# A residual layer with a split fp32 product on one Trainium2 core: another place in the order for stores, for one cast of W and for two products

## Chip, cores and metric

The kernel runs on one core of one Trainium2 chip. The metric is the device time of one execution in microseconds (us), as the median of several runs. Lower is better.

## What is computed

The reference, cut to what matters (B = 4 rows, L = 1024, D = 512, `cond` has 256 columns, W is 1536 x 512):

```python
hidden = concatenate([cond, cond], axis=-1)                    # (4, 512)
x_mean = mean(x, axis=1, keepdims=True)                        # (4, 1, 512)
fused = concatenate([x, x_mean * ones_L, hidden[:, None, :] * ones_L], axis=-1)
relation = relu(einsum('bld,do->blo', fused, W) + b)
out = x + relation
```

The first 512 rows of W multiply x itself. The other 1024 rows multiply something that is the same for all 1024 positions of a row of the batch, so the kernel computes that part once for each of the four rows, as a bias of 512 numbers.

## The kernel before

**Tiles.** x is cut into 32 tiles t of 128 positions by 512 columns, eight to a batch row. A product tile needs x transposed, in four chunks j of 128 columns. To get fp32 accuracy, x and W are both split into a high part and a rest, `hi` and `lo`, `w_hi` and `w_lo`, and each chunk takes three matmuls (task `p{t}.{j}.{n}`, L365): n = 0 is hi by w_hi, n = 1 lo by w_hi, n = 2 hi by w_lo. That makes 12 matmuls of 512 columns for a tile, collected in one of five PSUM banks `po`. `p{t}.{j}` is all three at once.

**Where the parts come from.** The four chunks of W arrive in buffer x0 (tasks `W0` to `W3`); ScalarE's queue issues the first, SyncE the others. `wh{j}` (L218 on VectorE, L216 on ScalarE) casts a chunk to w_hi, `wl{j}` (L222) subtracts to get w_lo. For the first four tiles TensorE makes the transposes itself (`T{u}.{j}`, L262) from a regrouped copy (`y`, L237 or L235); for the later ones VectorE transposes blocks of a second load of x (`Z` loads into buffers z, transposes L264). `h{u}.{j}` on ScalarE (L271) casts to hi and adds up the sums that the mean needs, as an ACTIVATE and a read of its accumulator. `l{u}.{j}` (L277) on VectorE or GpSimd subtracts to get lo.

**The way out.** A finished bank is copied to a buffer `o` (`K`, L432, L430 or L440), gets its bias (`b`, L436 on GpSimd) and the relu (`r`, L447 on ScalarE), and is added to the plain x tile (`F`, L454, on GpSimd or VectorE). The last four tiles start their banks from the bias and finish in one step on VectorE (`F`, L423, and the halves of the last tile `F31r`, `F31l`, L403). `S{t}` stores the tile from the x buffer.

**Plain x and its buffers.** `X{g}.{h}` loads pairs of plain tiles for the final addition. Eight groups g of four tiles share six buffers: group 6 goes where group 0 was, and group 7 where group 1 was. So X6.0 has to wait until the stores S0 and S1 have landed, X6.1 for S2 and S3, X7.0 for S4 and S5, X7.1 for S6 and S7.

**Order.** Nothing is scheduled automatically. The table `ORDER` (from L22) lists every task, and each engine issues its tasks in just that order, with semaphore waits between engines. An engine that waits holds back everything behind it. All `X`, `Z`, `M`, `S` tasks and W1 to W3 are DMAs that SyncE issues (L146), in one queue. The program gives eight semaphores to the DMAs in turn, so that an issue also waits for the landing of the one eight places ahead of it.

Of the kernel before, what the change touches and what calls it, by code (L numbers as in the profile page):

```python
# [21 lines left out]
ORDER = """  # L22
W0@a X0.0 fill X0.1 relu fill X0.2 fill W1 fill W2 fill fill W3 fill y0.2@d y0.0@d X0.3 y0.1@d fill Z4.0 wh0r@d T0.0
fill wh0l@d h0.0 T0.2 wl0r@d Z4.1 T0.3 T0.1 p0.0.0 y1.0@d h0.2 Z4.3 wl0l@d y1.1@a T1.0 T1.1 l0.0@d h0.1 p0.0.2
y2.0@d Z4.2 y2.1@a T1.2 p0.0.1 h1.0 T1.3 T2.0 h1.1 T2.2 l1.0@d T2.1 wh1@d T2.3 p1.0.2 h2.1 p1.0.1 wl1@d h2.3 p1.1.0
p0.1.0 h1.3 wh2@d p1.0.0 h1.2 p0.1.2 l0.2@d h0.3 p1.2.0 l1.2@d h2.0 l2.1@d p2.1.2 wh3@a l2.3@d p2.1.0 Z5.3 l0.1@d
p1.1.2 l2.0@d p1.2.1 wl2@d p0.2.1 p2.1.1 y3.0@a p2.3.0 wl3@d p1.3.0 Z5.2 h2.2 p0.1.1 l1.1@d p0.3.0 l0.3@d p1.2.2
l1.3@d p0.3.2 l2.2@d p2.3.2 p1.1.1 Z5.0 p2.0.2 p1.3.1 T3.2 p2.0.0 T3.3 p2.3.1 p2.2.0 Z5.1 p2.2.1 p2.2.2 T3.0 T3.1
p0.2.2 h3.0 p2.0.1 h3.3 p0.2.0 C l3.0@d p1.3.2 h3.1 B p3.0 h3.2 l3.1@d K1@a l3.3@d V l3.2@d p3.1 T4.0 K2@a M1 T4.1
p3.2 h4.0 M0 h4.1 p0.3.1 l4.0@d p3.3 T4.2 l4.1@p p6.0 M3 T4.3 h4.2 p7.0 K0@a l4.2@d p4.1 h4.3 M2 p6.2 l4.3@p p4.0  # L30
Z6.3 T5.2 Z6.0 p5.0 to0 T5.1 Z6.2 K3@d p4.2 h5.1 t2 p7.2 as0 T5.0 h5.2 p6.3 t3 T5.3 h5.0 p5.1 h5.3 l5.0@d Z6.1 ac0@p
p7.3 t0 l5.2@d p4.3 ac1@p t1 p6.1 c0.0 K4@a Z8.1 p5.3 l5.3@p c0.1 p9.0 Z7.2 m0.0 p5.2 l5.1@p m0.1 p8.2 Z7.3 K5@a
m0.2 K6@a p8.3 m0.3 p10.0 Z7.1 p11.1 f0 p8.1 Z7.0 fa0 p11.0 vh0 T6.3 p11.2 X4.1 vl0 h6.3 X2.1 p10.1 T6.2 l6.3@p p7.1
Z8.0 T6.1 pb0 T6.0 p8.0 bc0@a Z8.2 as1 p9.1 b5@p K8@d h6.2 p9.2 Z8.3 h6.1 l6.2@d p9.3 b0@p h6.0 c1.0 p10.3 K7@a Z9.1
c1.1 to1 p13.2 K9@a l6.1@p m1.0 p13.3 l6.0@d p11.3 b3@p T7.1 p13.1 K11@a m1.1 r0@a p14.1 Z9.2 b1@p m1.2 h7.1 p10.2
T7.0 p14.0 X1.0 b4@p K10@a X1.1 T7.3 h7.0 p14.2 m1.3 l7.1@p Z9.0 p15.1 l7.0@d f1 p12.2 h7.3 fa1 b6@p p13.0 T7.2 vh1
p16.0 l7.3@p Z10.3 h7.2 vl1 p14.3 Z9.3 r1@a T8.1 p12.1 F0@p T8.0 h8.1 Z10.0 p15.2 T8.3 pb1 b7@p l7.2@d p16.3 bc1@a
as2 p15.3 K13 h8.3 F1@p p12.0 T8.2 r7@a p12.3 X3.1 h8.0 b8@p X2.0 p18.1 h8.2 K12 S0 p18.2 r3@a c2.0 to2 Z10.2 r4@a
p17.3 b2@p c2.1 r8@a p18.0 m2.0 F3@p p18.3 r2@a K14 r5@a p17.1 m2.1 r12@a l8.3@p S3 p16.1 m2.2 Z10.1 p17.2 X5.1 m2.3
F2@p p19.1 S1 l8.0@d f2 p15.0 l8.1@p r6@a fa2 p17.0 K15 X4.0 vh2 p19.2 F5@p T9.0 p19.3 vl2 h9.0 p19.0 F4@p T9.1  # L40
p20.1 l8.2@d b11@p pb2 p16.2 bc2@a h9.1 p20.2 K16 b10@p as3 p20.3 T9.2 p20.0 K17 h9.2 l9.1@p p21.2 r13@a l9.2@d
r17@a p22.0 T9.3 F7@p X6.0 K18 p21.1 h9.3 X3.0 S5 c3.0 F8@p p22.3 r10@a S4 T10.2 p21.0 S2 S7 K20 l9.3@p p21.3 h10.2
X5.0 l9.0@d r18@a p23.2 T10.1 F6@p p23.0 T10.3 p25.1 K21 b9@p h10.3 p22.2 T10.0 h10.1 p23.3 c3.1 h10.0 X6.1 p26.0
X7.0 r15@a F18@d r9@a p25.3 to3 K19 F10@p r14@a p22.1 m3.0 r19@a p26.3 m3.1 F9@p p26.2 m3.2 p24.1 m3.3 F17@p S9
p25.2 S6 K22 f3 S18 p24.0 F12@p S8 fa3 p25.0 vh3 F19@d p23.1 r20@a X7.1 F13@p p24.3 r22@a S10 K23 S17 p27.1 vl3
r23@a l10.3@p p26.1 l10.0@d r11@a pb3 F23@d p27.2 bc3@a F11@p l10.2@d S23 P28 p27.0 S19 K25 p24.2 S12 F15@p K26 P30
S11 p28.0 K24 P31l p27.3 r16@a F22@d S15 P29 S13 p30.3 F14@p r21@a S22 p28.2 r26@a F21@d S14 p28.3 l10.1@p K27 S21
p29.3 r27@a p29.2 F26@d r25@a p29.0 F20@d P31r S26 r24@a F27@d p30.1 S20 F25@d p28.1 S27 F24@p S25 p31.2l F28 p29.1
S28 F16@p p31.0l F29 p31.3l p30.0 S29 S24 p30.2 S16 p31.1r F30 p31.3r p31.2r S30 p31.0r p31.1l F31r F31l S31r S31l
""".split()  # L50


# [436 lines left out]
```

## Time and profile before

| what | value |
|---|---|
| median of 3 runs | 103.57 us |
| the three runs | 103.57, 104.98, 101.28 us |
| the profiled execution: its time | 101.22 us |
| the profiled execution: span from first to last instruction | 99.5 us |
| TensorE (PE) busy | 95.0 us, 96% of the span |
| VectorE (DVE), ScalarE (ACT), GpSimd (POOL) busy | 80.2, 58.2, 65.1 us |
| granted TensorE clock | full in all 40 slices |
| moved by DMA | 27.36 MB, 275 GB/s on the mean |

The profiled execution takes 1.7 us more than its span. PE is TensorE's matmuls, PEld its weight loads, SP is SyncE. The times in a row of the timeline count from the span's start.

### The profile page before, as it was taken

To read this page: it belongs to the slowest core of one execution; us is meant where nothing else is said; L and a number is where in the kernel's file an instruction comes from. 1 tells how busy PE (TensorE), PEld (TensorE's weight loads), DVE (VectorE), ACT (ScalarE), POOL (GpSimd) and SP (SyncE) were. 2 spreads that over 40 slices of the span, in tenths; PEclk is the share of its full clock that TensorE was granted. 3 is DMA by queue.
4 is the path that set the end of the run, shared out by engine and by line. 5 is a ranking of instruction groups with operands and counts; after the bars stand their busy time and mean duration, and the time that the engine had idled before them with its cause. 6 is when DMAs were issued, how large, how long until landed. Compare 5 with 4: busy or idle time off the path is not lost.

```text
span 99.5 us, 1446 instructions
## 1 busy us (share of the span) xinstructions
PE 95.0 (96%) x425; PEld 76.2 (77%) x425; DVE 80.2 (81%) x144; ACT 58.2 (58%) x153; POOL 65.1 (65%) x65
## 2 busy tenths in 40 slices
PE   6999999999999999999999999999999999999960
PEld 2466888778888888888888888888888888888850
DVE  1559807999897967999988999799999989699550
ACT  4297308659316549487899745677593587952000
POOL 5000000549940249999999999999979999967400
PEclk9999999999999999999999999999999999999999
DMA  2999999999999999999999999848999589999993
GB/s 43 376 375 239 210 199 212 278 394 314 222 209 212 215 254 269 209 223 275 259 212 242 328 294 268 308 133 264 390 315 366 208 275 285 404 406 406 398 385 123
DMA packets 25361, 27.36 MB, mean 275 GB/s; under 512 B 1413, under 2 KB 16009, under 8 KB 25354
## 3 DMA queue, kind: packets, MB, share of 16 engines
q1 hardware_dynamic: 25210, 27.01, 100.8%
q10 hardware_dynamic: 144, 0.26, 0.7%
q8 instruction: 3, 0.05, 0.2%
q14 instruction: 4, 0.03, 0.1%
HBM read 18.88 MB, written 8.39 MB: 274 GB/s over the span
## 4 chain that ended last, share of the span: by engine, by line
PE 93%; ACT 2%; DVE 1%; issue 0%
PE po L365 87%; PE po L132 4%; ACT hi L271 1%; PE acc L343 1%; DVE x L403 1%; ACT o L235 1%; PE po L262 0%; DVE lo L277 0%; PE acc L262 0%; PE px L262 0%; DVE warm L123 0%; DVE one L124 0%
## 5 line engine op out<-in xcount | busy, mean ns | idle before, releaser
L365 PE MATMUL po<-w_hi,lo 128*128 128x512 f32 (+1 forms) x132 | 50.6, 386 | 0.1
L365 PE MATMUL po<-w_lo,hi 128*128 128x512 f32 (+1 forms) x132 | 50.5, 385 | 0.0
L365 PE MATMUL po<-w_hi,hi 128*128 128x512 f32 (+1 forms) x132 | 50.4, 386 | 0.0
L277 POOL TENSOR_TENSOR lo<-xT,hi 128x512 fp32r<-128x512 f32 x14 | 18.6, 1335 | 23.5 <-ACT hi L271 23.5
L365 PEld LDWEIGHTS po<-w_hi,lo 128*128 128x128 f32 x132 | 24.9, 188 | 5.7 <-DVE lo L277 0.7
L365 PEld LDWEIGHTS po<-w_hi,hi 128*128 128x128 f32 x132 | 24.7, 188 | 5.3 <-issue 0.4
L365 PEld LDWEIGHTS po<-w_lo,hi 128*128 128x128 f32 x132 | 24.8, 188 | 4.7
L454 POOL TENSOR_TENSOR x<-o,x 128x512 f32<-128x512 f32 x19 | 26.3, 1406 | 1.5 <-ACT o L447 1.5
L447 ACT ACTIVATE o<-o 128x512 f32<-128x512 f32 x28 | 16.2, 620 | 1.6 <-DVE o L440 1.3
L436 POOL TENSOR_TENSOR o<-o,bias 128x512 f32<-128x512 f32 x12 | 15.5, 1309 | 1.4 <-ACT bias L347 1.4
L271 ACT ACTIVATE hi<-px 128x512 fp32r<-128x512 f32 (+1 forms) x20 | 9.9, 495 | 4.9 <-DVE px L264 2.6
L319 DVE SCALAR_TENSOR_TENSOR acc<-w_mean,tot,acc 128x512 f32<-128x512 f32 x16 | 12.0, 750 | 0.6
L440 DVE TENSOR_TENSOR o<-po,bias 128x512 f32<-128x512 f32 x16 | 10.7, 677 | 1.7 <-PE po L365 1.7
L277 DVE TENSOR_TENSOR lo<-px,hi 128x512 fp32r<-128x512 f32 (+1 forms) x20 | 10.9, 558 | 1.1 <-ACT hi L271 1.0
L271 ACT ACTIVATE hi<-xT 128x512 fp32r<-128x512 f32 x14 | 8.8, 627 | 3.0 <-DVE xT L264 3.0
L264 DVE STREAM_TRANSPOSE px<-z 128x512 f32<-128x512 f32 x14 | 9.9, 707 | 0.0
L264 DVE STREAM_TRANSPOSE xT<-z 128x512 f32<-128x512 f32 x14 | 9.6, 690 | 0.2
L432 ACT ACTIVATE o<-po 128x512 f32<-128x512 f32 x10 | 5.6, 599 | 5.6 <-PE po L365 5.6
L454 DVE TENSOR_TENSOR x<-o,x 128x512 f32<-128x512 f32 x9 | 8.0, 914 | 0.9 <-ACT o L447 0.9
L303 DVE SCALAR_TENSOR_TENSOR acc<-wc,cT,acc 128x512 f32<-128x512 f32 x8 | 6.0, 746 | 0.3
L132 PE MATMUL po<-warm 128*128 128x512 bf16 x9 | 4.1, 614 | 1.0 <-DVE one L124 1.0
L327 ACT ACTIVATE fold<-acc 64x512 f32<-64x512 f32 x4 | 2.4, 597 | 4.4 <-DVE acc L319 4.4
(53 smaller groups left out, 59.4 us busy)
## 6 DMA issues: line engine op xcount, KB each, us to landing
out_dram<-x SPq DMA_DIRECT2D x31, 256.0 KB, 4.0
z<-in_x_dram SPq DMA_DIRECT2D x28, 256.0 KB, 8.0
x<-in_x_dram SPq DMA_DIRECT2D x14, 512.0 KB, 6.5
x<-in_x_dram SPq DMA_DIRECT2D x4, 256.0 KB, 3.9
x<-in_L_cond_W_dram SPq DMA_DIRECT2D x1, 1024.0 KB, 7.6
w_mean<-in_L_cond_W_dram SPq DMA_DIRECT2D x4, 256.0 KB, 7.4
x<-in_L_cond_W_dram SPq DMA_DIRECT2D x3, 256.0 KB, 4.1
x<-in_L_cond_W_dram ACTq DMA_DIRECT2D x1, 256.0 KB
```

Of the source, the lines that this page charges most:

```text
L132: nc.tensor.matmul(ps_o[2], lhsT=warm, rhs=warm.rearrange("p (o d) -> p o d", o=1).to_broadcast([P, 4, P]), start=True, stop=True,)
L264: nc.vector.transpose(xT.rearrange("p (n q e) -> p n q e", q=Q // E, e=E), zs[z_of(u)][:, : n * NQ].rearrange("p n (q j e) -> p n j q e", ...
L271: nc.scalar.activation(his[buf][:, col : col + m], xT, AF.Copy, accum_out=sums[:, r, j, s : s + 1])
L277: nc_of[e].tensor_tensor(los[buf][:, col : col + m], xT, his[buf][:, col : col + m].bitcast(F32), ALU.subtract)
L303: nc.vector.scalar_tensor_tensor(acc, wc[:, k], cT[:, k, r : r + 1], acc, ALU.mult, ALU.add)
L319: nc.vector.scalar_tensor_tensor(acc, w_mean[:, j, :], tot[:, r, j : j + 1], acc, ALU.mult, ALU.add)
L365: nc.tensor.matmul(v, lhsT=a[:, col : col + P], rhs=m, start=WAYS[t] != "I" and key not in done, stop=done.count(key) == 3 * J - 1, skip_g ...
L432: nc.scalar.activation(o, bank(t), AF.Copy)
L436: nc_of[e].tensor_tensor(o, o, biases[r], ALU.add)
L440: nc.vector.tensor_tensor(o, bank(t), biases[r], ALU.add)
L447: nc.scalar.activation(o, o, AF.Relu)
L454: nc_of[e].tensor_tensor(x_tile(t), o, x_tile(t), ALU.add)
```

## The change

Only the table `ORDER` is changed. It has 28 lines instead of 27, so all later code stands one line further down.

- On VectorE, `wh1` (the cast of W's second chunk to w_hi) stands ahead of `l1.0` (lo of tile 1's first chunk) instead of behind it.
- On TensorE, `p1.1.0` and `p0.1.0`, which need that w_hi, stand ahead of `p1.0.1`, which needs that lo.
- On SyncE, stores from S2 on stand in the order in which their tiles are finished. S2, S5 and S4 stand ahead of the loads X6.0 and X3.0; X5.0, X6.1 and X7.0 stand behind S7 as before; of the later stores several change places with each other, and X7.1 now stands behind S8, S6, S18 and S10.

In the text of the table every store moves to just behind its `F`, which moves it on SyncE only where it passes another DMA.

```diff
-fill wh0l@d ... h1.1 T2.2 l1.0@d T2.1 wh1@d T2.3 p1.0.2 h2.1 p1.0.1 wl1@d h2.3 p1.1.0
-p0.1.0 h1.3 wh2@d p1.0.0 ...
+fill wh0l@d ... h1.1 T2.2 wh1@d l1.0@d T2.1 T2.3 p1.0.2 h2.1 p1.1.0 p0.1.0 p1.0.1
+wl1@d h2.3 h1.3 wh2@d p1.0.0 ...
...
-... X4.0 vh2 p19.2 F5@p ... F4@p ... F7@p X6.0 ... X3.0 S5 c3.0 F8@p ... S4 ... S2 S7 ... X5.0 ... X6.1 ... X7.0 ...
+... X4.0 S2 vh2 p19.2 F5@p S5 ... F4@p S4 X6.0 X3.0 ... F7@p S7 X5.0 X6.1 X7.0 ... F8@p S8 ...
```

VectorE near 6 us of the program, before: a copy for tile 2's transposes (`y2.0`), lo of tile 1 chunk 0, then the casts and subtractions of W's chunks 1 and 2.

```order
L237 COPY o10_115<-x2_65 128x256
L277 TENSOR_TENSOR lo1_91<-acc_143,hi1_76 128x128
L218 CAST w_hi_72<-x0_63 128x512
L222 TENSOR_TENSOR w_lo_73<-x0_63,w_hi_72 128x512
L218 CAST w_hi_72<-x0_63 128x512
```

And after:

```order
L238 COPY o10_115<-x2_65 128x256
L219 CAST w_hi_72<-x0_63 128x512
L278 TENSOR_TENSOR lo1_91<-acc_143,hi1_76 128x128
L223 TENSOR_TENSOR w_lo_73<-x0_63,w_hi_72 128x512
L219 CAST w_hi_72<-x0_63 128x512
```

The first cast has passed the subtraction that makes lo; the rest stands as it did.

TensorE at the same place, before: from `p1.0.2` to `p1.2.0` (po1 and hi1 are tile 1's, po0 and hi0 tile 0's).

```order
L365 MATMUL po1_137<-w_lo_73,hi1_76 128x512
L365 MATMUL po1_137<-w_hi_72,lo1_91 128x512
L365 MATMUL po1_137<-w_hi_72,hi1_76 128x512
L365 MATMUL po0_136<-w_hi_72,hi0_75 128x512
L365 MATMUL po1_137<-w_hi_72,hi1_76 128x512
L365 MATMUL po0_136<-w_lo_73,hi0_75 128x512
L365 MATMUL po1_137<-w_hi_72,hi1_76 128x512
```

And after:

```order
L366 MATMUL po1_137<-w_lo_73,hi1_76 128x512
L366 MATMUL po1_137<-w_hi_72,hi1_76 128x512
L366 MATMUL po0_136<-w_hi_72,hi0_75 128x512
L366 MATMUL po1_137<-w_hi_72,lo1_91 128x512
L366 MATMUL po1_137<-w_hi_72,hi1_76 128x512
L366 MATMUL po0_136<-w_lo_73,hi0_75 128x512
L366 MATMUL po1_137<-w_hi_72,hi1_76 128x512
```

The product with lo has gone from second to fourth place, and two products with the moved cast's w_hi stand ahead of it.

SyncE from X4.0 to X7.0, before (x2 is the buffer of tiles 0 to 3 and later of 24 to 27, x3 that of tiles 4 to 7 and later of 28 to 31, x5 that of tiles 12 to 15, x1 of tiles 20 to 23):

```order
L146 DMA x0_63<-in_x_dram 128x2x512
L146 DMA x2_65<-in_x_dram 128x2x512
L146 DMA x5_68<-in_x_dram 128x2x512
L146 DMA out_0_dram<-x3_66 128x512 x2
L146 DMA out_0_dram<-x2_65 128x512
L146 DMA out_0_dram<-x3_66 128x512
L146 DMA x1_64<-in_x_dram 128x2x512
L146 DMA x2_65<-in_x_dram 128x2x512
L146 DMA x3_66<-in_x_dram 128x2x512
```

And after:

```order
L147 DMA x0_63<-in_x_dram 128x2x512
L147 DMA out_0_dram<-x2_65 128x512
L147 DMA out_0_dram<-x3_66 128x512 x2
L147 DMA x2_65<-in_x_dram 128x2x512
L147 DMA x5_68<-in_x_dram 128x2x512
L147 DMA out_0_dram<-x3_66 128x512
L147 DMA x1_64<-in_x_dram 128x2x512
L147 DMA x2_65<-in_x_dram 128x2x512
L147 DMA x3_66<-in_x_dram 128x2x512
```

Three stores of 256 KB (S2, S5, S4) have passed two loads of 512 KB (X6.0, X3.0); S7 and the three loads behind it keep their places.

## Rows read from the trace of the kernel before

**Rows 1.** The page's busy times, and its DMA slices (40 slices of 2.49 us)

```profile
PE 95.0 (96%) x425; PEld 76.2 (77%) x425; DVE 80.2 (81%) x144; ACT 58.2 (58%) x153; POOL 65.1 (65%) x65
...
DMA  2999999999999999999999999848999589999993
```

**Rows 2.** The chain that ended last: start us, us, what

```profile
7.43 5.61 PE po L365 x22
...
49.85 12.92 PE po L365 x57
...
82.26 13.43 PE po L365 x69
...
95.72 0.78 DVE x L403 x2
```

**Rows 3.** Timeline of VectorE from 5.6 us: start us, us, what [idle before]

```profile
5.71 0.28 DVE L237 COPY o<-x 128x256 f32<-128x256 f32 x1
7.09 0.29 DVE L277 TENSOR_TENSOR lo<-acc,hi 128x128 fp32r<-128x128 f32 x1 [1.10 <-ACT hi L271]
7.30 0.42 DVE L218 CAST w_hi<-x 128x512 fp32r<-128x512 f32 x1
7.75 0.69 DVE L222 TENSOR_TENSOR w_lo<-x,w_hi 128x512 fp32r<-128x512 f32 x1
8.36 0.42 DVE L218 CAST w_hi<-x 128x512 fp32r<-128x512 f32 x1
```

**Rows 4.** Timeline of TensorE's matmuls from 6.8 us

```profile
6.90 0.48 PE L365 MATMUL po<-w_lo,hi 128*128 128x512 f32 x1
7.43 0.50 PE L365 MATMUL po<-w_hi,lo 128*128 128x512 f32 x1
7.86 0.94 PE L365 MATMUL po<-w_hi,hi 128*128 128x512 f32 x3
8.64 0.39 PE L365 MATMUL po<-w_lo,hi 128*128 128x512 f32 x1
8.93 0.47 PE L365 MATMUL po<-w_hi,hi 128*128 128x512 f32 x1
```

**Rows 5.** Timeline of ScalarE: the read of the accumulator that ends `h1.1`

```profile
6.84 0.21 ACT L271 ACTIVATION_READ_ACCUMULATOR hi<-acc 128x1 f32 x1
```

**Rows 6.** SyncE's issue of W1 to W3, and W's time from issue to landing

```profile
2.10 1.92 SPq L146 DMA_DIRECT2D x<-in_L_cond_W_dram  x3
...
x<-in_L_cond_W_dram SPq DMA_DIRECT2D x3, 256.0 KB, 4.1
```

**Rows 7.** SyncE's queue: its longest waits (us in total, times, longest)

```profile
SPq L146 <- DMA out_dram<-x: 9.6, 4, 4.8
SPq L146 <- POOL x L454: 6.9, 5, 2.8
...
SPq L485 <- DMA out_dram<-x: 1.3, 1, 1.3
```

**Rows 8.** Stretches: us, then busy us (x instructions) by engine, PEclk, DMA share, GB/s

```profile
64.00:66.00 2.00, 2.00 (x10) 1.66 (x9) 1.82 (x4) 1.59 (x6) 2.00 (x3) 1.00 0.32 88
...
77.00:79.20 2.20, 2.20 (x12) 1.81 (x11) 2.13 (x4) 0.94 (x2) 2.20 (x3) 1.00 0.51 187
...
82.00:97.00 15.00, 14.04 (x74) 11.89 (x72) 11.89 (x18) 6.29 (x12) 9.69 (x7) 1.00 1.03 379
97.00:98.20 1.20, 0.00 (x0) 0.00 (x0) 0.00 (x0) 0.00 (x0) 0.00 (x0) 1.00 0.74 254
```

**Rows 9.** X7.1, loads of 512 KB (us to landing), the last issue (S31l), the addition of tile 30

```profile
80.47 0.39 SPq L146 DMA_DIRECT2D x<-in_x_dram  x1
...
x<-in_x_dram SPq DMA_DIRECT2D x14, 512.0 KB, 6.5
...
96.60 0.40 SPq L146 DMA_DIRECT2D out_dram<-x  x1
...
94.29 0.69 DVE L423 SCALAR_TENSOR_TENSOR x<-po,x 128x512 f32<-128x512 f32 x1 [1.02 <-PE po L365]
```

More of the change, by code (lines that the diff above doesn't have):

```diff
@@ L24 @@
 fill wh0l@d h0.0 T0.2 wl0r@d Z4.1 T0.3 T0.1 p0.0.0 y1.0@d h0.2 Z4.3 wl0l@d y1.1@a T1.0 T1.1 l0.0@d h0.1 p0.0.2
[L25 to L48, printed above, removed]
@@ L49 @@
-S28 F16@p p31.0l F29 p31.3l p30.0 S29 S24 p30.2 S16 p31.1r F30 p31.3r p31.2r S30 p31.0r p31.1l F31r F31l S31r S31l
+y2.0@d Z4.2 y2.1@a T1.2 p0.0.1 h1.0 T1.3 T2.0 h1.1 T2.2 wh1@d l1.0@d T2.1 T2.3 p1.0.2 h2.1 p1.1.0 p0.1.0 p1.0.1
+wl1@d h2.3 h1.3 wh2@d p1.0.0 h1.2 p0.1.2 l0.2@d h0.3 p1.2.0 l1.2@d h2.0 l2.1@d p2.1.2 wh3@a l2.3@d p2.1.0 Z5.3
+l0.1@d p1.1.2 l2.0@d p1.2.1 wl2@d p0.2.1 p2.1.1 y3.0@a p2.3.0 wl3@d p1.3.0 Z5.2 h2.2 p0.1.1 l1.1@d p0.3.0 l0.3@d
+p1.2.2 l1.3@d p0.3.2 l2.2@d p2.3.2 p1.1.1 Z5.0 p2.0.2 p1.3.1 T3.2 p2.0.0 T3.3 p2.3.1 p2.2.0 Z5.1 p2.2.1 p2.2.2 T3.0
@@ new lines @@
+T3.1 p0.2.2 h3.0 p2.0.1 h3.3 p0.2.0 C l3.0@d p1.3.2 h3.1 B p3.0 h3.2 l3.1@d K1@a l3.3@d V l3.2@d p3.1 T4.0 K2@a M1
+T4.1 p3.2 h4.0 M0 h4.1 p0.3.1 l4.0@d p3.3 T4.2 l4.1@p p6.0 M3 T4.3 h4.2 p7.0 K0@a l4.2@d p4.1 h4.3 M2 p6.2 l4.3@p
+p4.0 Z6.3 T5.2 Z6.0 p5.0 to0 T5.1 Z6.2 K3@d p4.2 h5.1 t2 p7.2 as0 T5.0 h5.2 p6.3 t3 T5.3 h5.0 p5.1 h5.3 l5.0@d Z6.1
+ac0@p p7.3 t0 l5.2@d p4.3 ac1@p t1 p6.1 c0.0 K4@a Z8.1 p5.3 l5.3@p c0.1 p9.0 Z7.2 m0.0 p5.2 l5.1@p m0.1 p8.2 Z7.3
+K5@a m0.2 K6@a p8.3 m0.3 p10.0 Z7.1 p11.1 f0 p8.1 Z7.0 fa0 p11.0 vh0 T6.3 p11.2 X4.1 vl0 h6.3 X2.1 p10.1 T6.2 l6.3@p
@@ new lines @@
+p7.1 Z8.0 T6.1 pb0 T6.0 p8.0 bc0@a Z8.2 as1 p9.1 b5@p K8@d h6.2 p9.2 Z8.3 h6.1 l6.2@d p9.3 b0@p h6.0 c1.0 p10.3 K7@a
+Z9.1 c1.1 to1 p13.2 K9@a l6.1@p m1.0 p13.3 l6.0@d p11.3 b3@p T7.1 p13.1 K11@a m1.1 r0@a p14.1 Z9.2 b1@p m1.2 h7.1
+p10.2 T7.0 p14.0 X1.0 b4@p K10@a X1.1 T7.3 h7.0 p14.2 m1.3 l7.1@p Z9.0 p15.1 l7.0@d f1 p12.2 h7.3 fa1 b6@p p13.0
+T7.2 vh1 p16.0 l7.3@p Z10.3 h7.2 vl1 p14.3 Z9.3 r1@a T8.1 p12.1 F0@p T8.0 h8.1 Z10.0 p15.2 T8.3 pb1 b7@p l7.2@d
+p16.3 bc1@a as2 p15.3 K13 h8.3 F1@p p12.0 T8.2 r7@a p12.3 X3.1 h8.0 b8@p X2.0 p18.1 h8.2 K12 S0 p18.2 r3@a c2.0 to2
@@ new lines @@
+Z10.2 r4@a p17.3 b2@p c2.1 r8@a p18.0 m2.0 F3@p p18.3 r2@a K14 r5@a p17.1 m2.1 r12@a l8.3@p S3 p16.1 m2.2 Z10.1
+p17.2 X5.1 m2.3 F2@p p19.1 S1 l8.0@d f2 p15.0 l8.1@p r6@a fa2 p17.0 K15 X4.0 S2 vh2 p19.2 F5@p S5 T9.0 p19.3 vl2
+h9.0 p19.0 F4@p S4 X6.0 X3.0 T9.1 p20.1 l8.2@d b11@p pb2 p16.2 bc2@a h9.1 p20.2 K16 b10@p as3 p20.3 T9.2 p20.0 K17
+h9.2 l9.1@p p21.2 r13@a l9.2@d r17@a p22.0 T9.3 F7@p S7 X5.0 X6.1 X7.0 K18 p21.1 h9.3 c3.0 F8@p S8 p22.3 r10@a T10.2
+p21.0 K20 l9.3@p p21.3 h10.2 l9.0@d r18@a p23.2 T10.1 F6@p S6 p23.0 T10.3 p25.1 K21 b9@p h10.3 p22.2 T10.0 h10.1
@@ new lines @@
+p23.3 c3.1 h10.0 p26.0 r15@a F18@d S18 r9@a p25.3 to3 K19 F10@p S10 X7.1 r14@a p22.1 m3.0 r19@a p26.3 m3.1 F9@p S9
+p26.2 m3.2 p24.1 m3.3 F17@p S17 p25.2 K22 f3 p24.0 F12@p S12 fa3 p25.0 vh3 F19@d S19 p23.1 r20@a F13@p S13 p24.3
+r22@a K23 p27.1 vl3 r23@a l10.3@p p26.1 l10.0@d r11@a pb3 F23@d S23 p27.2 bc3@a F11@p S11 l10.2@d P28 p27.0 K25
+p24.2 F15@p S15 K26 P30 p28.0 K24 P31l p27.3 r16@a F22@d S22 P29 p30.3 F14@p S14 r21@a p28.2 r26@a F21@d S21 p28.3
+l10.1@p K27 p29.3 r27@a p29.2 F26@d S26 r25@a p29.0 F20@d S20 P31r r24@a F27@d S27 p30.1 F25@d S25 p28.1 F24@p
@@ L50 @@
+p31.2l F28 p29.1 S28 F16@p p31.0l F29 p31.3l p30.0 S29 S24 p30.2 S16 p31.1r F30 p31.3r p31.2r S30 p31.0r p31.1l F31r
+F31l S31r S31l
 """.split()
```

## The prediction

> **What bounds the kernel now.** I read the page's busy times first, then the chain of waits, then the timelines of the places that the change touches, then SyncE's queue. TensorE is busy for 95.0 of the 99.5 us [rows 1]. Busy alone would not prove a bound, so the chain has to: from 7.43 us to 95.7 us it is made of TensorE's own work, one piece after the other, with no wait between [rows 2]. One of its pieces has 57 products in 12.92 us, which is 0.227 us for each [rows 2], and I use that as the step from one product to the next. Behind the last product come the two halves of the last addition, to 96.50, and the last store. So the time falls only where TensorE stands still ahead of 7.43 us or shortly behind it, or at the very end. All of the middle, from some 9.5 us on, is full.
>
> Where does TensorE stand still early? The reader should look at the starts: 6.90, 7.43, 7.86 (three products), 8.64, 8.93 [rows 4]. Six steps lie between 6.90 and 8.93, which at 0.227 would be 1.36 us; they take 2.03. VectorE explains it. It ends a copy at 5.99, stands idle for 1.10 us until `l1.0` starts at 7.09, and only then casts W's second chunk (7.30 to 7.72), subtracts (7.75 to 8.44) and casts the third (8.36 to 8.78) [rows 3]. The idle time ends with ScalarE: the read that completes `h1.1` lasts to 7.05 [rows 5].
>
> SyncE's queue is the other thing to look at. Its longest waits are for stores to land, 9.6 us in four waits, the longest 4.8, and for GpSimd's additions, 6.9 us [rows 7]. While it waits, the DMA engines run dry: share 0.32 from 64 to 66 us and 0.51 from 77 to 79.2. From 82 to 97 us they are full, at 379 GB/s [rows 8].
>
> **The cast and the two products.** Nothing is added or removed: a cast of 0.42 us changes places with a subtraction of 0.29, and two products with one. Has W's second chunk landed when VectorE comes to it? W1 is the first of three issues from 2.10 us, and such a load takes 4.1 us [rows 6], so it is there at about 6.2. The trace does not show that moment itself: the upper bound is 7.30, where the cast started before without waiting for a DMA [rows 3]. I take 6.2. Then the cast runs from 6.25 to 6.67, in idle time, and delays nothing: `l1.0` still starts at 7.09.
>
> Now TensorE. `p1.1.0` needs that cast and `h1.1` (7.05), so it can start at about 7.2 instead of 7.86. `p0.1.0` follows at 7.43, `p1.0.1` at 7.66 (its lo is ready at 7.38, as before), `p1.0.0` at 7.88. `p0.1.2` needs `wl1`. That subtraction no longer has the cast in front of it, so it starts 0.21 behind `l1.0` (the step that the cast had before), at 7.30, and ends at 7.99: the product starts at about 8.15 instead of 8.64. `p1.2.0` needs `wh2`, which starts 0.61 behind `wl1` as before (7.75 to 8.36 [rows 3]), at 7.91, and ends at 8.33. Before, the product started 0.15 behind that cast's end (8.78 to 8.93 [rows 3, 4]); so it now starts at 8.48. The gain at this point is 8.93 - 8.48 = 0.45 us.
>
> Its bounds: without any wait the product would start at 6.90 + 1.36 = 8.26, so at most 0.67 us can be won; if W1 lands at 7.30, the cast stands where it stood and nothing is won. What is late next is VectorE's own row of work, cast, subtraction, cast, which now starts 0.45 earlier as a whole. The work behind it (subtractions, casts, the transposes of later tiles) is the same, and moves with it. It meets DMAs only at the transposes of z, where no wait for one shows before, so that 0.45 less is probably covered. If it isn't, that much of the gain goes back, and the floor is again nothing.
>
> Behind 9.5 us TensorE's row has no hole in it, so what is won early is still won at 95.7.
>
> **The stores.** On SyncE three stores pass two loads. Each of the stores waits for its addition on GpSimd; the loads behind them wait for S0 and S1 to land anyway, and that is the 4.8 us wait [rows 7]. So S2, S5 and S4 go out inside it. That moves transfers from the full stretch to the dry one. Does it move the end? No product waits for a plain load or a store, only the additions and the buffers do, and the chain has none of them until the last addition. I cost the stores at nothing as long as TensorE's row covers them. The cover is gone for one that is in the last stretch: the last store is issued at 96.60, its issue ends at 97.00, and SyncE's closing wait takes another 1.3, so it has landed at 98.3, after 1.7 us [rows 7, 9]. Was it in a queue? From 97.0 to 98.2 the engines are busy for 0.74 x 1.2 = 0.89 us [rows 8]; the last two halves, 256 KB, are 0.69 us of that at 379 GB/s, so up to 0.2 us may have been other stores ahead of it. Bounds of the gain at the end: 0 to 0.2; less than nothing is excluded, since fewer transfers are left for this stretch. I take 0, nearest to the last two halves filling it alone.
>
> The Trainium skill, "DMA: Bandwidth & Descriptors" (Anatomy of one DMA), speaks against the stores' part: it puts about 2 us of each DMA down to a fixed cost, most of it the receipt of the write, and by it 128 KB would take an estimated 2.3 us even in an empty queue. The trace has 1.7 from issue to landing, less than that, so by this page no queue is left at the end for the new order to empty, and the sum would be the same 0.45.
>
> **The sum.** 0.45 us early, 0 in the middle, 0 at the end. The profiled execution took 101.22 us, so 100.77 for one like it; its span would be 99.05. The runs differ much more than that: 101.28, 103.57 and 104.98, with a median of 103.57, which would become 103.1. The profile belongs to the short ones. I predict the middle of all four executions, (101.28 + 103.57) / 2 = 102.43, less 0.45: 102.0 us. A measurement of this kernel can tell about 2% from no change, so this is no change.
>
> **Rivals.**
>
> *The stores decide the long executions.* If what makes an execution 2 us longer is slower transfers, the full stretch from 82 us on ends last there, not TensorE. For it: that stretch is full for 15 us, and the dry ones have 0.68 x 2.0 + 0.49 x 2.2 = 2.4 us of unused transfer time [rows 8], which the new order can use for stores that before came late. A median like 103.57 would then come back by about 2.3 beside the 0.45: 100.8 us. Against it: in the trace that there is, TensorE ends last, and the extra time of the others could as well lie at the first load.
>
> *The gain is lost.* W1 lands later than I think, or the transposes meet their loads. Then the time stays at 102.4. If W1 lands well after 7.1, the cast even holds `l1.0` back, and `p1.0.1` can't fill the gap: one step, 0.23 us, so 102.7. For it: the landing is from a median of three loads. Against it: before, the cast started at once.
>
> *The loads come too late: slower.* X7.1 is needed by tile 30's addition at 94.29. Before, it was issued at 80.47 and by the typical 6.5 us had landed at 87.0 [rows 9]. It now stands behind S10, and X6.0 and X3.0 behind three stores, each waiting for GpSimd. From a landing at 94.3 on, each us is a us at the end; 2.3 us beyond that give 104.3. Against it: that takes a landing 9.6 us later than before, and the stores that X7.1 needs to have landed go out earlier, not later. The same page of the Trainium skill (Latency and other measured facts) has HBM access at 0.2 us on average and 2 us under high load, so loads among stores may take some 1.8 us more by its figures; no run here shows that yet, and it leaves most of the 7.3 us of room.
>
> **Chances.** The forecast 0.69; the stores decide 0.12; the gain lost 0.13; the loads too late 0.06. Of the first and third, 0.02 may come out over 2% on either side by the spread of the executions alone. So faster by over 2%: 0.12 + 0.02 = 0.14; slower: 0.06 + 0.02 = 0.08; within: 0.78. The range: an execution like the profiled one with all bounds, 0.67 and 0.2, is at 100.35, and the longest run less the forecast's 0.45 at 104.5; I cut the top a little, as the median of several will seldom be its longest: 100.4 to 104.2.
>
> **What would show it.** In the timeline after: the cast of 0.42 us on VectorE starting at 6.2 to 6.3, `l1.0` still at 7.1, `p1.1.0` at 7.2, `p1.2.0` near 8.5, the last addition ending near 96.05, the span near 99.05. On SyncE: three stores issued ahead of 64 us, inside what was the 4.8 us wait, and a DMA share well over 0.32 from 64 to 66 and under 1 in part of 82 to 97. Wrong would be: a cast that waits for its DMA beyond 7 us; a new hole in TensorE's row between 9.5 and 95; a last addition that waits for a load; or a time under 100.3, which no step here can give.

## The result and the profile after

The changed kernel takes 101.19 us (median of 21 runs, 100.58 to 102.27), the kernel before, run beside it, 101.75 us (median of 21, 101.06 to 105.55). The ratio is 0.9933, with a 95% interval of 0.9909 to 0.9957: within 2%, and a little faster. The forecast was 102.0 us with a range of 100.4 to 104.2 and no change as the likeliest case. The ratio leaves out executions over 1.5% above a kernel's shortest, and since the stores turned out to touch just those, the number of runs over 102.3 us stands beside it from here on: 9 of 21 for the kernel before, none of 21 for the changed one.

The profiled execution of the changed kernel took 101.31 us, its span is 99.6. The page's busy times and DMA slices, which answer to [rows 1]:

```profile
PE 95.2 (96%) x425; PEld 76.7 (77%) x425; DVE 80.4 (81%) x144; ACT 58.3 (58%) x153; POOL 65.0 (65%) x65
...
DMA  2999999999999999999999899999999889998693
```

Nothing was added, so the busy times stand. The DMA slices differ: where before had dips to 4, 8 and 5 in the middle and nines to the end, there are eights and nines in the middle, and an 8 and a 6 near the end, where nothing but nines stood. The windows of [rows 8] say the same in numbers, with two more from the very end (us, busy us by engine, PEclk, DMA share, GB/s):

```profile
64.00:66.00 2.00, 2.00 (x11) 1.65 (x10) 1.82 (x4) 1.59 (x6) 2.00 (x3) 1.00 1.05 379
77.00:79.20 2.20, 2.20 (x11) 1.84 (x10) 2.13 (x4) 0.82 (x2) 2.20 (x2) 1.00 1.01 385
82.00:97.00 15.00, 14.16 (x74) 12.00 (x72) 12.00 (x18) 6.33 (x13) 9.80 (x7) 1.00 0.93 354
97.00:98.20 1.20, 0.00 (x0) 0.00 (x0) 0.00 (x0) 0.00 (x0) 0.00 (x0) 1.00 0.81 277
...
98.00:98.50 0.50, 0.00 (x0) 0.00 (x0) 0.00 (x0) 0.00 (x0) 0.00 (x0) 0.98 0.10 31
98.50:99.00 0.50, 0.00 (x0) 0.00 (x0) 0.00 (x0) 0.00 (x0) 0.00 (x0) 0.50 0.00 0
```

The share from 64 to 66 us has gone from 0.32 to 1.05, the one from 77 to 79.2 from 0.51 to 1.01; from 82 to 97 it has fallen from 1.03 to 0.93. SyncE's waits, which answer to [rows 7]:

```profile
SPq L147 <- DMA out_dram<-x: 6.5, 3, 3.0
...
SPq L486 <- DMA out_dram<-x: 1.3, 1, 1.3
```

The longest wait for a store to land is 3.0 us instead of 4.8, and the closing wait is still 1.3. The chain of waits, as in [rows 2]:

```profile
4.78 0.43 PE po L133
5.21 0.43 PE po L263 x2
...
82.38 13.43 PE po L366 x69
...
95.84 0.78 DVE x L404 x2
```

This is a riddle at first: the last addition starts at 95.84, 0.12 us later than before, though TensorE should have won 0.45. The timelines of VectorE and TensorE, as in [rows 3, 4], show where that went:

```profile
6.15 0.43 DVE L219 CAST w_hi<-x 128x512 fp32r<-128x512 f32 x1 [0.27 <-DMA x<-in_L_cond_W_dram]
7.46 0.29 DVE L278 TENSOR_TENSOR lo<-acc,hi 128x128 fp32r<-128x128 f32 x1 [0.88 <-ACT hi L272]
7.67 0.68 DVE L223 TENSOR_TENSOR w_lo<-x,w_hi 128x512 fp32r<-128x512 f32 x1
...
7.46 0.48 PE L366 MATMUL po<-w_lo,hi 128*128 128x512 f32 x1
7.77 0.63 PE L366 MATMUL po<-w_hi,hi 128*128 128x512 f32 x2
...
8.94 0.51 PE L366 MATMUL po<-w_hi,hi 128*128 128x512 f32 x1
```

From `p1.0.2` to `p1.2.0` it takes 8.94 - 7.46 = 1.48 us; before it took 2.03. But `p1.0.2` itself starts at 7.46, where before had 6.90. Nothing of the change stands ahead of it on TensorE. The chain's rows show where the time went: the two transposes at 5.21 took 0.43 us, 0.21 each, and the fill at 4.78 also 0.43. The first experiment is the same kernel once more, in which the same pieces took 0.22 and 0.27.

### The profile page after: what moved, and what is told of

It reads as the page before. It is cut to its first block, busy times and chain, and to the rows that moved or that the text cites. A ratio compares the mean times of both kernels' runs of the same rounds, so it can differ in the third digit from the quotient of the medians.

```text
span 99.6 us, 1451 instructions
## 1 busy us (share of the span) xinstructions
PE 95.2 (96%) x425; PEld 76.7 (77%) x425; DVE 80.4 (81%) x144; ACT 58.3 (58%) x153; POOL 65.0 (65%) x65
## 3 DMA queue, kind: packets, MB, share of 16 engines
q1 hardware_dynamic: 25210, 27.01, 100.2%
## 4 chain that ended last, share of the span: by engine, by line
PE 95%; DVE 1%; issue 0%
PE po L366 88%; PE po L133 4%; PE acc L344 1%; PE po L263 1%; PE px L263 1%; DVE x L404 1%; PE acc L263 1%; DVE warm L124 0%; DVE one L125 0%
```

## The experiments

There are twelve experiments in three groups. The ratio of each is to the kernel before, run beside it in the same group, where it had 5 of 11, 19 of 35 and 13 of 36 runs over 102.3 us.

### The changed kernel again, twice

No edit.

> The changed kernel again, as the yardstick for the two halves of the change. The first measurement gave 0.9933 of the time before. Theory A (the early cast and the two products carry the gain, by about 0.55 us from p1.0.2 to p1.2.0 as the trace after shows: 1.48 instead of 2.03 us) and theory B (the stores carry it, by an end that comes sooner after the last addition) both expect 0.991 to 0.996 again. In the trace both expect p1.0.2 to p1.2.0 within 1.45 to 1.55 us.

Measured: median 101.30 us (6 runs, 100.75 to 101.42), ratio 0.9956 (0.9919 to 0.9993). Its profiled execution took 100.75 us with a span of 99.1. First its chain, then its timeline:

```profile
4.78 0.27 PE po L133
5.04 0.22 PE po L263 x2
...
95.29 0.78 DVE x L404 x2
```

```profile
6.23 0.43 DVE L219 CAST w_hi<-x 128x512 fp32r<-128x512 f32 x1 [0.27 <-DMA x<-in_L_cond_W_dram]
7.09 0.29 DVE L278 TENSOR_TENSOR lo<-acc,hi 128x128 fp32r<-128x128 f32 x1 [0.43 <-ACT hi L272]
7.29 0.68 DVE L223 TENSOR_TENSOR w_lo<-x,w_hi 128x512 fp32r<-128x512 f32 x1
7.89 0.42 DVE L219 CAST w_hi<-x 128x512 fp32r<-128x512 f32 x1
...
6.90 0.48 PE L366 MATMUL po<-w_lo,hi 128*128 128x512 f32 x1
7.22 0.62 PE L366 MATMUL po<-w_hi,hi 128*128 128x512 f32 x2
7.67 0.39 PE L366 MATMUL po<-w_hi,lo 128*128 128x512 f32 x1
7.90 0.39 PE L366 MATMUL po<-w_hi,hi 128*128 128x512 f32 x1
8.12 0.40 PE L366 MATMUL po<-w_lo,hi 128*128 128x512 f32 x1
8.46 0.47 PE L366 MATMUL po<-w_hi,hi 128*128 128x512 f32 x1
```

Here the transposes take 0.11 us each, `p1.0.2` starts at 6.90 as in the trace of before, and this is the execution to hold against the prediction. `p1.2.0` starts 0.47 us earlier than before (8.46, 8.93 [rows 4]), and 0.43 of it is left at the end: the last halves of the addition start at 95.29 instead of 95.72 [rows 2] and end at 96.07. So the trace of after above is later by a slower stretch of TensorE ahead of the change (0.56 us at `p1.0.2`, 0.55 at the last addition), not by anything the change does.

The second time, in the third group:

> The changed kernel once more on this chip: 0.991 to 0.996 of before, median 101.0 to 101.4, longest under 102.4.

Measured: median 101.11 us (12 runs, 100.60 to 103.32), ratio 0.9958 (0.9922 to 0.9994), 2 of 12 over 102.3. The gain repeats, and so does its trace: `p1.0.2` at 6.94, `p1.2.0` at 8.43, the last addition from 95.26. The spread is much smaller than that of before but not wholly gone; "longest under 102.4" was missed.

### The early half alone, twice

```diff
-h1.1 T2.2 l1.0@d T2.1 wh1@d T2.3 p1.0.2 h2.1 p1.0.1 wl1@d h2.3 p1.1.0 p0.1.0 h1.3 wh2@d p1.0.0
+h1.1 T2.2 wh1@d l1.0@d T2.1 T2.3 p1.0.2 h2.1 p1.1.0 p0.1.0 p1.0.1 wl1@d h2.3 h1.3 wh2@d p1.0.0
```

> Only the cast and the two products are moved; SyncE's order is that of before. Theory A: the whole gain is here, 0.993 to 0.996 of before (0.45 to 0.67 us less), and p1.0.2 to p1.2.0 takes 1.45 to 1.55 us instead of 2.03. Theory B: 0.998 to 1.002, although the early stretch is shorter.

> The early half alone once more, for more runs. If the stores end last in most executions of before, an earlier TensorE alone gains little: shortest run 100.7 to 101.1 as in the changed kernel, but the median as before within 0.5 us, some runs over 103.5. If the early half acts by itself, median 0.4 to 0.6 us under that of before.

Measured: first median 103.08 us (6 runs, 101.32 to 108.70), ratio 1.0029 (0.9962 to 1.0096), 4 of 6 over 102.3; then median 101.36 (12 runs, 100.74 to 104.53), ratio 0.9969 (0.9936 to 1.0003), 4 of 12 over 102.3. The first is inconclusive; the second has the predicted 0.45 us (a ratio of 0.9956) within its interval, and also, at its very edge, no gain. Its median is 0.31 us under that of before, which is short of the 0.4 to 0.6 that was expected if this half acts by itself. The long executions stay either way: this half does nothing to them that shows.

The trace of the second run shows something else. TensorE, with `p1.0.2`, `p1.2.0` and the product behind it:

```profile
7.75 0.47 PE L365 MATMUL po<-w_lo,hi 128*128 128x512 f32 x1
...
9.22 0.50 PE L365 MATMUL po<-w_hi,hi 128*128 128x512 f32 x1
9.56 0.40 PE L365 MATMUL po<-w_lo,hi 128*128 128x512 f32 x1
```

Here TensorE is later still, and the new order brings the product behind `p1.2.0` to 9.56. The next kernel, which has the old order here, was caught with TensorE just as late, and reaches it at 9.59; the last addition starts at 96.10 here and at 96.09 there.

### The stores alone

```diff
-X4.0 X6.0 X3.0 S5 S4 S2 S7 X5.0 X6.1 X7.0 S9 S6 S18 S8 X7.1 S10 S17 S23 S19 S12 S11 S15 S13 S22
+X4.0 S2 S5 S4 X6.0 X3.0 S7 X5.0 X6.1 X7.0 S8 S6 S18 S10 X7.1 S9 S17 S12 S19 S13 S23 S11 S15 S22
```

(Here and below only the loads and stores of the order are written out.)

> Only the stores are moved; the early part is that of before. Theory A: no difference, 0.998 to 1.002; p1.0.2 to p1.2.0 still takes about 2.0 us, and the time from the end of the last addition to the end of the span is the 3.0 us of before within 0.1. Theory B: 0.993 to 0.996, with the time behind the last addition at 2.5 us or less.

Measured: median 101.56 us (6 runs, 101.06 to 101.60), ratio 0.9983 (0.9949 to 1.0018), none over 102.3. By the ratio the stores are worth nothing that shows, as predicted. But all six runs lie within 0.54 us, where the kernel before beside it goes from 101.11 to 105.71. Its timeline at the early place, which has the order of before:

```profile
7.45 0.29 DVE L277 TENSOR_TENSOR lo<-acc,hi 128x128 fp32r<-128x128 f32 x1 [1.46 <-ACT hi L271]
...
7.74 0.48 PE L365 MATMUL po<-w_lo,hi 128*128 128x512 f32 x1
...
9.29 0.47 PE L365 MATMUL po<-w_hi,hi 128*128 128x512 f32 x1
9.59 0.40 PE L365 MATMUL po<-w_lo,hi 128*128 128x512 f32 x1
```

From `p1.0.2` to `p1.2.0` it takes 1.55 us, where the trace of before has 2.03 [rows 4], with nothing changed there. `l1.0` starts 0.29 us ahead of `p1.0.2` here, and started 0.19 behind it before [rows 3, 4]: when TensorE itself is late, VectorE's row hides behind it and the hole is nearly closed already. So "still about 2.0 us" was missed, and in such an execution the early half has 0.03 us to win (9.59 - 9.56).

### One fill in the hole

```diff
-p1.0.2 h2.1 p1.0.1
+p1.0.2 fill h2.1 p1.0.1
```

> The kernel before with one more fill, a bf16 matmul of 512 columns without use, between p1.0.2 and p1.0.1, where TensorE stands still for some 0.2 us. Theory C (what the early hole costs is not only its length: a TensorE that stands still there gets less clock afterwards, so that filling the hole with anything helps): 0.993 to 0.997, and a full clock in more of the profiled time. Theory A: the hole is filled with nothing useful and the next product starts when its lo is there or up to 0.2 us later, 0.999 to 1.003.

Measured: median 102.12 us (6 runs, 101.01 to 103.83), ratio 0.9964 (0.9910 to 1.0018), 3 of 6 over 102.3. The interval leaves both theories open. The trace shows no gain (`p1.0.2` at 7.25, `p1.2.0` at 9.27, which is 2.02 us, 2.03 before), and the long executions stay, 3 of only 6, so standing still in the hole is not likely to make them. The useful part is an accident: the profiled execution is itself a long one, 102.85 us with a span of 101.2. Its order of loads and stores is that of before. Windows, then the timeline of VectorE's last addition and of SyncE's issues, then SyncE's waits for stores, the closing one last:

```profile
81.20:83.20 2.00, 2.00 (x11) 1.65 (x10) 1.97 (x4) 1.62 (x3) 2.00 (x3) 1.00 0.10 37
83.20:97.00 13.80, 13.19 (x70) 11.19 (x68) 11.03 (x16) 5.73 (x12) 8.84 (x6) 1.00 1.02 371
97.00:98.20 1.20, 0.00 (x0) 0.00 (x0) 0.00 (x0) 0.00 (x0) 0.00 (x0) 1.00 1.03 393
```

```profile
96.07 0.78 DVE L403 SCALAR_TENSOR_TENSOR x<-po,x 128x256 f32<-128x256 f32 x2 [0.74 <-PE po L365]
...
66.18 0.89 SPq L146 DMA_DIRECT2D x<-in_x_dram  x2
...
69.35 5.66 SPq L146 DMA_DIRECT2D x<-in_x_dram  x3
77.10 2.15 SPq L146 DMA_DIRECT2D out_dram<-x  x4
82.34 0.39 SPq L146 DMA_DIRECT2D x<-in_x_dram  x1
82.78 15.44 SPq L146 DMA_DIRECT2D out_dram<-x  x22
```

```profile
SPq L146 <- DMA out_dram<-x: 12.6, 4, 4.8
SPq L485 <- DMA out_dram<-x: 1.8, 1, 1.8
```

The last addition ends at 96.85. In the trace of the stores alone it ends at 96.87, so TensorE is as early here as there; but that span ends at 99.9, 3.0 us behind the addition (3.0 in the trace of before too, 99.5 - 96.5), and this one 4.3 behind it. So here the stores end last, not TensorE. The rows account for it: SyncE has issued its last store at 98.22 (82.78 + 15.44), 1.37 us behind the addition instead of 0.50 (97.00 [rows 9] - 96.50), and its closing wait is 1.8 us instead of 1.3.

What stands ahead of that is a SyncE that comes later at each load that reuses a buffer. X6.0 goes out at 66.18 (64.91 before), X6.1, which waits for S2 to land, at 74.11 (72.95 before), and X7.1 at 82.34 (80.47 [rows 9]) behind a stretch of 2 us in which the DMA engines are busy for 0.10 of it. The stores that SyncE waits for cost it 12.6 us in four waits, 9.6 before [rows 7]. From 83.2 us on the engines are full and stay full beyond 97, at 1.03, where before had 0.74 [rows 8]. That transfers were moved by this into a stretch without room fits all these rows, but it is read from one trace. The three loads X5.0, X6.1 and X7.0 are not what tells a long execution from a short one: here they take 5.66 us to issue, and in the short one of before

```profile
68.25 5.61 SPq L146 DMA_DIRECT2D x<-in_x_dram  x3
```

What tells these two apart is X7.1's wait for S6. A store's landing is recorded in 16 parts, as many as there are DMA engines. S6 is issued at 77.51 here, 15 of its parts have landed by 80.72, and the last lands at 82.33, 1.61 us behind; X7.1 goes out at once. Before, S6 was issued at 77.16 and all 16 parts landed between 80.17 and 80.45.

For comparison, SyncE's issues in the same places in the first repeat of the changed kernel:

```profile
60.25 2.49 SPq L147 DMA_DIRECT2D out_dram<-x  x3
65.74 0.90 SPq L147 DMA_DIRECT2D x<-in_x_dram  x2
...
67.85 1.55 SPq L147 DMA_DIRECT2D x<-in_x_dram  x3
...
78.00 0.39 SPq L147 DMA_DIRECT2D x<-in_x_dram  x1
```

S2, S5 and S4 are out from 60.25 us on, so S2 has landed before X6.1 comes up, the same three loads take 1.55 us, and X7.1 goes out at 78.00. This execution has late parts too: S2's last one lands at 67.57, 2.33 us behind the fifteenth. Nothing waits for it, as X6.1 goes out at 68.39.

### X7.1 later

```diff
-S8 X7.1 S10 S17 S23 S19 S12 S11 S15 S13 S22 S14
+S8 S10 S17 S23 S19 S12 S11 S15 S13 S22 X7.1 S14
```

> The kernel before with one move: the load X7.1, which waits for S6 and S7 to land, stands behind S22 instead of ahead of S10. Theory G (the stores from S10 on are held back in SyncE's queue by X7.1's wait, and the time varies with how late that wait ends): S10 and the stores behind it go out as their tiles are finished, the last store lands within 2.2 us of the last addition, and the runs lie together, median 101.5 to 101.7, longest under 102.4, where the kernel before has 101.8 to 102.0 and 105.7. Theory H (it is the first three stores, held back by X6.0's wait): the spread stays, median 102 or more, longest over 103.5. Theory K (the spread is TensorE's clock at the start): it stays as well, with spans that go with the granted clock.

Measured: median 102.48 us (12 runs, 101.98 to 103.97), ratio 1.0064 (1.0020 to 1.0108), 10 of 12 over 102.3. Theory G's median of 101.5 to 101.7 is missed: all twelve runs are later than that. But only 2 of 12 are over 103.0, where before beside it has 13 of 35, so that X7.1's wait has a part in the longest executions is not ruled out. The window of the end:

```profile
97.00:98.20 1.20, 0.00 (x0) 0.00 (x0) 0.00 (x0) 0.00 (x0) 0.00 (x0) 1.00 1.05 386
```

X7.1 goes out at 86.44, so its 512 KB move towards the end, and 97 to 98.2 us is full as in the long execution above. The span is 100.2, 3.9 us behind the end of the last addition at 96.32. So this place has a price of its own in every run.

### The first three stores alone, and the later ones alone

```diff
-X4.0 X6.0 X3.0 S5 S4 S2 S7
+X4.0 S2 S5 S4 X6.0 X3.0 S7
```

> Only S2, S5 and S4 ahead of X6.0 and X3.0; the later stores as before. Theory H: the runs lie together, median 101.5 to 101.7, longest under 102.4; X6.1 no longer waits for S2 (issue near 69 us instead of 73), and with it the whole queue behind comes sooner, X7.1 by about 1.5 us. Theory G: X7.1 still stands behind S9, which waits for its addition until 76.7, and S6 lands late, so X7.1 is issued at 80 us or later and some runs are over 103.5.

and, with these three where they were,

```diff
-S9 S6 S18 S8 X7.1 S10 S17 S23 S19 S12 S11 S15 S13 S22
+S8 S6 S18 S10 X7.1 S9 S17 S12 S19 S13 S23 S11 S15 S22
```

> Only the later stores in the order of finished tiles (S8, S6, S18, S10 ahead of X7.1, S9 behind it, and so on); X6.0 and X3.0 stand ahead of S5, S4 and S2 as before. Theory G: S6 goes out right behind its addition (near 72 to 74 us instead of 77), X7.1 is issued at 79 us or sooner, the runs lie together, median 101.5 to 101.7. Theory H: X6.1 still waits for S2 until 73 us and holds back S8, S6 and what follows, X7.1 is issued at 80 or later, and some runs are over 103.5.

Measured: the first three alone, median 101.58 us (12 runs, 101.24 to 102.21), ratio 1.0004 (0.9973 to 1.0035), none of 12 over 102.3. The later ones alone, median 102.10 (12 runs, 101.12 to 104.53), ratio 0.9980 (0.9928 to 1.0033), 6 of 12 over 102.3. It is the three stores that pass X6.0 which take the long executions away (before had 19 of 35 beside them); the rest of the new order does nothing that shows. In SyncE's timeline the three loads X5.0, X6.1, X7.0 take 1.57 us with the first three ahead:

```profile
68.67 1.57 SPq L146 DMA_DIRECT2D x<-in_x_dram  x3
```

and 5.39 us with only the later ones reordered:

```profile
68.32 5.39 SPq L146 DMA_DIRECT2D x<-in_x_dram  x3
```

That X7.1 would come 1.5 us sooner with the first three ahead was missed: in that trace it goes out at 80.03, against 80.47 before.

### Which of the three

```diff
-X4.0 X6.0 X3.0 S5 S4 S2 S7
+X4.0 S2 X6.0 X3.0 S5 S4 S7
```

> The kernel before with S2 alone ahead of X6.0 and X3.0; S5 and S4 stay behind them. Theory H1 (what counts is that X6.1 waits for S2's landing and holds back the queue until 73 us): X6.1 is issued near 69 us, the runs lie together, median 101.5 to 101.7, longest under 102.4. Theory H2 (what counts is that 768 KB of stores fill the dry stretch near 64 us): one of three stores fills 0.65 of 2 us, the spread is reduced by about a third only, some runs over 103.5, median about 102.

```diff
-X4.0 X6.0 X3.0 S5 S4 S2 S7
+X4.0 S5 S4 X6.0 X3.0 S2 S7
```

> The kernel before with S5 and S4 ahead of X6.0 and X3.0; S2 stays behind them. Theory H1: X6.1 still waits for S2's landing until 72 us or later, the queue behind it is held back, some runs over 103.5, median about 102 to 102.5. Theory H2: 512 KB of the 768 fill the dry stretch, two thirds of the spread go, median 101.6 to 101.8, longest under 103.

Measured: S2 alone, median 101.56 us (12 runs, 100.75 to 104.32), ratio 0.9993 (0.9948 to 1.0037), 3 of 12 over 102.3. S5 and S4 alone, median 101.74 (12 runs, 100.94 to 103.45), ratio 1.0011 (0.9978 to 1.0044), 2 of 12. Before had 13 of 36 beside them, so with 12 runs each neither count is clear of it, and neither theory is met. How the effect divides between S2's earlier landing (X6.1 goes out at 68.99 with S2 alone, at 71.73 with S5 and S4 alone) and the transfers moved into the dry stretch stays open.

### Both, for a better version

The changed kernel with X7.1 behind S22.

```diff
-S18 S10 X7.1 S9 S17 S12 S19 S13 S23 S11 S15 S22
+S18 S10 S9 S17 S12 S19 S13 S23 S11 S15 S22 X7.1
```

> The changed kernel with X7.1 behind S22 as well. If theory G holds, nothing holds back a store any more and the end hangs on TensorE alone: 0.990 to 0.996 of before, the runs within 100.7 and 101.5, which differ only by where TensorE's clock becomes full. If X7.1's wait no longer matters in the changed kernel, the same as that: 0.993 to 0.996. If the later load is late for tile 30, a hole ahead of the last additions and 1.00 or more.

Measured: median 101.42 us (12 runs, 101.02 to 102.84), ratio 0.9963 (0.9928 to 0.9998), 1 of 12 over 102.3. That is not better than the changed kernel (0.9933, 0.9956 and 0.9958 in its three measurements), and the longest run missed the 101.5 that was expected.

### All runs side by side

| order of the loads and stores | kernels | runs over 102.3 us |
|---|---|---|
| as before around X6.0 | before, early half, fill, X7.1 later, later stores | 46 of 103, 8 of 18, 3 of 6, 10 of 12, 6 of 12: 73 of 151 |
| part of the three ahead of X6.0 | S2 alone, S5 and S4 alone | 3 of 12, 2 of 12: 5 of 24 |
| all three ahead | changed, stores alone, first three, changed with X7.1 later | 2 of 39, 0 of 6, 0 of 12, 1 of 12: 3 of 69 |

The line at 102.3 us was drawn when the runs were known, just above the two longest of the changed kernel's first measurement (102.27). At 103.0 us the three rows have 48 of 151, 3 of 24 and 1 of 69. The kernel with X7.1 later, whose runs are shifted as a whole, can be left out: the first row is then 63 of 139 at 102.3 and 46 of 139 at 103.0.

Only one long execution has a trace. For the others there is the span and the mean granted clock. In the traces the only stretch with a recorded clock below 1.00 lies behind the last product (the two rows of 98 us above: it falls to 0.50, which is 1.2 of 2.4 GHz). If that holds for all, a mean below 1.00 gives the moment of the fall: for the trace of after, 2 x 0.006 x 99.6 = 1.2 us at half, so from 98.4, and its rows have it at 98.5. For the longest run of all (108.70 us, the early half; span 107.0, clock 0.969) it gives 6.6 us at half, so a fall at 100.4; for the 27 runs of before over 103 us beside the experiments, falls between 98.5 and 101.8. In the seven traces whose span reaches the fall, it lies between 98.5 and 101.0, with last additions that start between 95.5 and 96.1. The falls of the long runs lie in about the same place. So they ask for no late TensorE, though they don't exclude one that is late by a us or two, and TensorE was through by then in executions whose span goes on to 104 and 107. That fits stores that end last; it is worked out, not shown by a trace.

## Why the prediction was right, and where it wasn't

**The bound.** Right for the executions of the usual length. The chain of all three traces of the changed kernel runs through TensorE's own work to the last addition, with no wait, and its last piece is as long as before (69 products in 13.43 us, in one trace 13.44).

**The cast and the two products.** Right to some hundredths, in the execution in which TensorE was as quick as in the trace of before. W1's landing ended VectorE's wait at 6.23 (it was taken as 6.2, with the cast from 6.25); `l1.0` still at 7.09; `p1.1.0` at 7.22 (7.2), `p1.0.1` at 7.67 (7.66), `p1.0.0` at 7.90 (7.88), `wl1` at 7.29 (7.30), `p0.1.2` at 8.12 (8.15), `wh2` at 7.89 (7.91), `p1.2.0` at 8.46 (8.48). The last addition ended at 96.07 (96.05), the span is 99.06 (99.05) and the time 100.75 (100.77). What was won early meets no wait on its way; neither reason that I gave for a lost gain, W1 late or the transposes in the way, came true.

What I took for granted is that every execution has the hole of the one trace. It hasn't. With `p1.0.2` at 6.90 the hole cost 0.47 us (8.93 - 8.46), with 7.74 only 0.03 is left of it, by the two traces above. And at the same early `p1.0.2` it varies too: in the traces of the kernel with X7.1 later and of that with the later stores alone, both with the old order here, `p1.2.0` starts at 8.71 and 8.66 instead of 8.93, so that against 8.46 some 0.2 is left. In these traces 0.45 is near the upper end of what the early half gives, not its middle. That the one profiled execution of before had a large hole was luck.

The three ratios of the changed kernel, 0.9933, 0.9956 and 0.9958, are 0.68, 0.45 and 0.43 us of some 101.5. These are as large as the upper end or larger, so the stores may have a share in them; that is not shown. The runs of each half alone (0.9983 for the stores, 0.9969 for the early half in the second measurement, both with 1.0 in their interval) don't separate it.

**The stores, nothing in the middle and at the end.** Not refuted for executions like the profiled one: 0.9983 for the stores alone and 1.0004 for the first three, both with 1.0 in their interval. The transfers did move as said, and the closing wait is still 1.3 us [rows 7]. That fewer of them are left for the end holds in the first repeat (share 0.37 from 97 to 98.2 us, 0.74 before [rows 8]) and not in the trace of after (0.81). The span ends 3.0 us behind the last addition in all three, so nothing was won at the end. The Trainium skill's section that the prediction sets beside this ("DMA: Bandwidth & Descriptors", Anatomy of one DMA) gives its fixed cost for DMAs that GpSimd issues. SyncE's last store of 128 KB landed in 1.7 us by the trace of before, less than the 2.3 estimated from it, and the measurement decides.

**The sum's level.** It was 0.8 us too high. I took the middle of four executions, 102.43, for the kernel before; its 21 runs have a median of 101.75, and less 0.45 that is 101.3, against 101.19 measured. The three runs that I had were one short and two long ones.

**What failed: the cover over the stores.** "I cost the stores at nothing as long as TensorE's row covers them", and the rival in which the stores decide the long executions had a chance of 0.12, with the words against it that "the extra time of the others could as well lie at the first load". In the long execution that has a trace it lies at the end: TensorE is through at the usual time, the engines are full beyond 97 us, and the last store is late, the end 4.3 us behind the last addition instead of 3.0. The orders with all of S2, S5 and S4 ahead have nearly no such executions (3 in 69 runs). So this rival's mechanism holds in the one long execution that can be looked into, of 102.85 us. That the order of the stores decides most of the 46 long ones in 103 runs of the kernel before is what the counts say; by which steps it does so in those up to 105.7 us no trace shows. The size of its price, 2.3 us, fits the runs that went (103 runs of before have 35 from 103 to 105.7 us, 39 runs of the changed kernel have one), but not the time that it was given, 100.8: it supposed that a long execution would be the typical one.

**The loads too late.** This did not come true. X6.0 goes out later than before, 0.83 us in the first repeat (65.74 against 64.91) and 2.15 in the trace of after (67.06). But X7.1 goes out at 78.00 and 78.93 instead of 80.47; S6, for which it waits, goes out at 71.19 in the first repeat instead of 77.16. No addition waits for a load.

## What to carry to other kernels

Where one queue carries loads that reuse a buffer and stores that free one, a load that waits for a store to land holds up every finished store behind it: put these ahead of it, and look at the DMA share in the dry stretches ahead of a full end. Look at all runs as well as at one trace: that of a short execution showed TensorE as the bound, and said nothing of the 46 of 103 runs that took longer. The gain of a cast moved into idle time can be computed to some hundredths from the starts in two timelines, but it holds for that execution: take the hole from several traces before it is taken for the mean.

## What the hardware showed that was not expected

TensorE reaches its full rate at different moments in executions of one program. The fills start at 0.97 us in every trace, but the two transposes near 5 us step by 0.11 us in one trace of the changed kernel and by 0.21 in the other, and `p1.0.2` starts at 6.90 or 7.46; in the traces of the stores alone and of the first three stores, whose programs ahead of it are those of before, at 7.74 and 7.67. Each trace also records from when on the full clock was granted: from 4.76 us in the trace of before and in the first repeat, from 6.32 in that of after, from 6.94 and 6.79 in those of the stores alone and of the first three. Ahead of that there is no record, and a view counts a stretch without one as 1.00, so the full slices in the table of before don't speak for the first microseconds. The steps do: ahead of these moments they are about twice as long as behind them (0.43 us for a fill at 4.78 in the trace of after, 0.227 for the products later), as they would be at 1.2 of 2.4 GHz. The later moment moves `p1.0.2` by up to 0.84 us between these traces (6.90 to 7.74), more than the early half of the change gains, and decides how much that half gains. Why the moment differs is open.

A store's landing can be late though nearly all engines are idle: for 2 us, from 81.2 to 83.2 in the long execution, the share is 0.10, and up to 82.34 X7.1 waits for the last of the 16 parts of a store of 256 KB issued 4.8 us before. Such late parts come in some executions and not in others. In the first repeat the last part of 26 of SyncE's loads and stores lands over 1 us behind the fifteenth, in one by 2.8 us; in the trace of before none of those issued from 10 us on does, and the largest distance is 0.9. What makes a part late is not shown.
